# Two transformer layers in one kernel: order of the attention's small products, last down products row by row, first projections in two banks

## The chip, the cores and the metric

The kernel runs on one core of one Trainium2 chip. The metric is the device time of one execution in microseconds (us). Three runs of the kernel before took 1893.55, 1894.83 and 1896.32 us; the median is 1894.83. One further execution was recorded by the hardware profiler; all durations of single instructions come from it.

The core has five engines that run side by side and wait for each other through semaphores: PE multiplies matrices[...], DVE, ACT and POOL work elementwise, and SP issues DMA transfers.

## What is computed

Two layers, each with an attention-like part and a feed-forward part (FFN) that both read the same normalised input and are both added to x. The change touches the second layer only:

```
xn = _layernorm(x)
x = x + _L1_attn_ref(xn, ...) + _L1_ffn_ref(xn, ...)

# attention: b = 2, l = 1024, 16 heads of 32
qkv = x @ W_qkv.T + b_qkv
scores = einsum('bqhe,bkhe->bhqk', q, k) / sqrt(32), causal
attn = softmax(scores)
out = einsum('bhqk,bkhe->bqhe', attn, v) @ W_out.T + b_out

# FFN: 512 -> 2048 -> 512
h = silu(x @ w_gate) * (x @ w_up)
h_sparse = h with the two largest of each four |h| kept
out = h_sparse @ w_down
```

Everything is float32. A float32 product appears in the trace as two matmul instructions.

## The kernel before

The tokens are four blocks of 512 rows (`x1[0..3]`). The first layer ends at about 704 us; the second layer's attention runs from there to about 1283 us, its FFN to the end.

**Order of work.** Between `start = mark()` and `in_program_order(start)` (L1137 to L1154) each engine executes its instructions exactly in the order in which the Python code issues them. The same holds for the FFN from L1175 on. So moving a call in the Python code moves its instructions in every engine's queue.

**PSUM.** `ps_bank(name, which)` gives one of two single banks; `ps_wide(name)` gives one of three double banks, in strict rotation. A new tile waits until the last reader of the same bank or double bank is done.

**Projections.** `piece` (L826) builds a product of four chunks as two parts; its second part ends with `done`, which empties the bank: `project` (q and k) by ACT at L854, `values` by DVE at L872, `project_out` by DVE at L1027. The bank number is `(behind_steps or 1) % 2`. `behind_steps` is None until the attention's loop is over, so up to then every piece uses bank 1 (bank 0 holds the attention's output `o`); after the loop the two banks alternate. The first four pieces (L1133) run ahead of the loop.

**Attention.** A unit is a batch entry and a group of four heads, 8 units in all. The softmax needs each row's maximum first, so scores are computed twice: `maxima` (L881, tile `m`, rows on partitions) forms them 13 steps ahead, DVE adds the causal mask on the diagonal (L897) and reduces them to `tops` (L898). `larger` (L905) merges the two column halves of rows 512 to 1023. `shift_part` (L910) splits the negated maxima into three bf16 parts, and `shift_rows` (L922) turns them by four transposes on PE (tile `px`) and copies them with DVE (L932) into `neg`. `weights` (L934, tile `s`) forms the transposed scores (L943), adds `neg` by a product with ones (L949), takes the exponential on ACT (L960) and clears the masked corner on POOL (L965). `gather` (L974, tile `o`) multiplies with v (L985) and adds the weights up in `acc` (L993: POOL, from step 83 on DVE); it runs one step behind `weights`. When half j of a unit is done, `total` (L1000, tile `w`) sums `acc` over partitions by a product with ones, ACT copies the sum to `inv`, and `divide` (L1012) takes the reciprocal in four quarters on DVE and multiplies once on POOL (L1017).

The loop has 96 steps (12 per unit: 4 for j = 0, 8 for j = 1) and 13 ahead of them. One step n issues, in this order: `weights`; what is listed in `middle`; `gather` of the step before; (a projection part where n < 0); `maxima` of step n + 13; one projection part if one is ready; what is listed in `fixed`. For unit u, `shift_rows` is in `fixed` at 12u - 6 and 12u + 2, `larger` in `middle` at 12u - 1, `total` in `fixed` at 12u + 7 and 12u + 15, and its four `divide` one, one, two and three steps later.

**FFN.** Each of 8 groups has two gate-and-up units (`gate_up`), then `sparsify` (L1237: one ACT and eleven DVE instructions per half), then the down product. Seven groups use a 2x2 block scheme with seven products instead of eight (`down`, L1292, for each half of the rows; 8 matmul instructions of 256 columns each) whose inputs are sums: of weights by `down_weights` (POOL, L1219 to L1223; L1222 overwrites the quarter w12), of hidden values by `down_hidden` (DVE, L1232 to L1235). Several products of one half accumulate in the same bank, and DVE adds the bank to x1 between them (L1322). The last group uses plain row products, `row_down` (L1357: one block of 128 rows, 8 matmul instructions of 512 columns), which store their rows at once. Work that finds no place between the units is in `tail`: five products of the last-but-one group's half 0, all seven of its half 1, then the eight row products of the last group, with that group's `sparsify` steps (`some_steps`) in between.

Of the kernel before, what the change touches and what calls it, by code (L numbers as in the profile page):

```python
# [9 lines left out]
F32 = mybir.dt.float32  # L10
# [5 lines left out]
P = 128  # L16
B, S, D = 2, 1024, 512
N = B * S
TT = 512
# [16 lines left out]
def two_layers(ctx: ExitStack, tc: tile.TileContext, t: dict, out: bass.AP):  # L36
# [718 lines left out]
    with tc.tile_pool(name="b", bufs=1, reuse_waits="tile") as b:  # L755
# [67 lines left out]

        behind_steps = None

        def piece(name, lhs, rhs, done):  # L826


            got = []

            def part(n):
                if n == 0:
                    nonlocal behind_steps
                    if behind_steps is not None:
                        behind_steps += 1
                    got.append(ps_bank(name, (behind_steps or 1) % 2))
                for k in (2 * n, 2 * n + 1):
                    nc.tensor.matmul(  # L838
                        got[0], lhs(k), rhs(k), start=(k == 0), stop=(k == KC - 1)
                    )  # L840
                if n:
                    done(got[0])

            return [(part, 0), (part, 1)]
# [200 lines left out]

        rest, fixed, middle = [], {}, {}

# [3 lines left out]
        def put_mid(n, *what):  # L1051

            middle.setdefault(n, []).append(what)

        for u in range(len(units)):

            for half in range(2):
                n = per * u - ahead + (3, 11)[half]
                if half:
                    put_mid(n + 1, larger, u)  # L1060
                for m in range(3):
                    put_mid(n + 2 + m, shift_part, u, half, m)
                put(n + 4, shift_rows, u, half)
            if u:
                lo = per * (u - 2) if u > 1 else -ahead
                for x in range(4):
                    rest.append((lo, per * u - ahead - 1, project(u, x // 2, x % 2)))
            if u > 1:
                put(per * (u - 2) - 1, load_qk, units[u][1])
            for j in range(2):  # L1070
                put(min(per * u + 8 * j + 7, per * len(units) + 2), total, u, j)
        for x in range(4):
# [45 lines left out]
        def what_is_fixed(n):  # L1118
            for f, *args in fixed.pop(n, ()):
                f(*args)  # L1120
                if f == total:
                    for q in range(4):
                        put(n + 1 + (q * 2 // 3 if n < len(second) else 0), divide, *args, q)

# [8 lines left out]
        for x in range(4):  # L1133
            for f, *args in project(0, x // 2, x % 2):
                f(*args)
        behind = None
        start = mark()  # L1137
        for n in range(-ahead, len(second)):
# [3 lines left out]
            if behind is not None:  # L1142
                gather(*behind)
            behind = now
            if n < 0:
                one_part(n)
# [8 lines left out]
        gather(*behind)  # L1155
        behind_steps = 0
        n = len(second)
# [18 lines left out]
    with tc.tile_pool(name="c", bufs=1, reuse_waits="tile") as c_:  # L1176
# [34 lines left out]
        def down_weights(n, last):  # L1211
# [64 lines left out]
        held_d = {}  # L1276
        behind_units = False

        def bank_for(n, half, m):

            if not behind_units:
                return ps_bank(f"d{m}_{n}_{half}", (m + half) % 2)
            if m in (0, 3):
                held_d["pair"] = ps_wide(f"d{m}_{n}_{half}")
            return held_d["pair"][:, m in (1, 4), :]

        def residual(n, half, i, e):
# [4 lines left out]
        def down(n, half, m):  # L1292
# [3 lines left out]
            s2, s3, s4 = sd[n, half]  # L1296
            t1, t2, t4 = td[n]
# [59 lines left out]
        def row_down(n, i, j):  # L1357

            block = 2 * units[2 * n][0] + i
            bank = ps_bank(f"dr_{n}_{i}_{j}", i)  # L1360
            for r in range(4):
# [5 lines left out]
            nc.vector.tensor_add(x, x, bank)  # L1367
            row = block * TT + j * P
            nc.sync.dma_start(out=out[row : row + P, :], in_=x)

        for n in range(groups - 1):
# [6 lines left out]
            for last in range(2):  # L1378
                put1(u - 1, 3 + last, down_weights, n, last)
            for half, at in enumerate(((8, 11), ()) if end else (range(4, 11), range(11, 18))):  # L1380
                steps = list(sequence(n, half))
# [4 lines left out]
                tail += steps  # L1386
            put1(u, 3, down_hidden, n, 0)
            if not end:
# [24 lines left out]
        for n, (pb, g, half) in enumerate(units):  # L1413
# [33 lines left out]
            if n + 2 < len(units):  # L1447
                load_gu(n + 2)
        behind_units = True
        for f, *args in tail:  # L1450
# [73 lines left out]
```

## Time and profile before

The profiled execution took 1895.49 us; its span, from the first to the last instruction, is 1893.8 us, which leaves 1.7 us around it. Busy time in each stage, from the profile by windows:

| window (us) | what runs | PE busy | DVE | ACT | POOL | granted PE clock |
|---|---|---|---|---|---|---|
| 0 to 704 | first layer | 682.24 | 305.60 | 139.67 | 187.67 | 1.00 |
| 704 to 722 | first four projections | 14.80 | 0.45 | 2.52 | 0.00 | 1.00 |
| 722 to 1260 | attention's loop | 515.50 | 339.87 | 198.45 | 323.70 | 0.99 |
| 1260 to 1283 | last output projections | 23.00 | 7.77 | 0.58 | 6.22 | 1.00 |
| 1283 to 1824 | FFN units | 534.18 | 381.61 | 118.96 | 194.54 | 1.00 |
| 1824 to the end | tail | 55.65 | 36.74 | 5.04 | 6.71 | 0.91 |

PE is the busiest engine in every stage. Its idle time is largest in the tail, where it is busy for 55.65 of 70 us. The granted clock is the share of PE's full speed that the chip allowed; below 1.00 the same matmul takes longer.

### The profile page before, as it was taken

The numbers are of one execution on the slowest core, as the hardware profiler recorded it, in microseconds if no ns is written. First come the engines' busy times: TensorE is split into PE (matmuls) and PEld (weight loads), VectorE is DVE, ScalarE is ACT, GpSimd is POOL, SyncE is SP. The second block draws the span as 40 slices with busy tenths as digits, with TensorE's granted clock in tenths as the row PEclk, the third lists the DMA queues.
The fourth block names the chain that finished last, engine by engine and source line by source line (L and its number), as shares of the span: only waits on it lengthen the run. The fifth ranks groups of instructions, "written<-read, shape, count | busy, mean of one in ns | idle before, by whom it ended". The sixth has DMA issues, their size and how long they took to land.

```text
span 1893.8 us, 17968 instructions
## 1 busy us (share of the span) xinstructions
PE 1825.4 (96%) x6988; PEld 851.4 (45%) x6988; DVE 1072.0 (57%) x1430; ACT 465.2 (25%) x660; POOL 718.8 (38%) x638
## 2 busy tenths in 40 slices
PE   7999999999999999999999999899999999999988
PEld 4444444444444443333333333334455555555554
DVE  3774443334533235655666656652768678668664
ACT  2321121112221112334333333421212212211220
POOL 4222233114441101366667657732243344344310
PEclk9999999999999999999999999999999999999999
DMA  6121111001110100000000000011111102201001
GB/s 234 39 78 34 34 34 34 23 22 47 37 34 22 34 6 23 1 12 12 1 12 12 24 11 12 24 45 29 38 29 49 56 22 78 78 22 56 34 0 45
DMA packets 29460, 68.06 MB, mean 36 GB/s; under 512 B 3392, under 2 KB 11584, under 8 KB 27840
## 3 DMA queue, kind: packets, MB, share of 16 engines
q1 hardware_dynamic: 28656, 66.61, 11.0%
q8 instruction: 56, 0.92, 0.2%
q10 hardware_dynamic: 720, 0.30, 0.1%
q14 instruction: 28, 0.23, 0.0%
HBM read 62.70 MB, written 4.19 MB: 35 GB/s over the span
## 4 chain that ended last, share of the span: by engine, by line
PE 88%; DVE 5%; issue 2%; ACT 2%; POOL 1%; DMA 0%; SPq 0%; DVEq 0%; ACTq 0%; POOLq 0%
PE p_a L177 20%; PE p_c L177 19%; PE acc L621 12%; PE d L1308 9%; PE pq L838 6%; PE m L890 4%; PE s L943 4%; PE o L985 3%; PE po L838 2%; PE pv L838 2%; PE dr L1362 1%; DVE tops L898 1%; PE w L1005 1%; POOL acc L993 1%; DVE m L897 1%
## 5 line engine op out<-in xcount | busy, mean ns | idle before, releaser
L993 POOL TENSOR_TENSOR acc<-acc,pt 128x1024 f32<-128x1024 f32 (+3 forms) x138 | 233.7, 1715 | 0.0
L621 PE MATMUL acc<-w2h,h 128*128 128x512 f32 x512 | 230.1, 594 | 3.1 <-DVE y L533 1.8
L898 DVE TENSOR_REDUCE tops<-m 128x2 f32<-128x1024 f32 (+2 forms) x192 | 180.8, 955 | 59.3 <-PE m L890 54.7
L634 DVE TENSOR_TENSOR x<-x,acc 128x512 f32<-128x512 f32 x128 | 86.1, 685 | 174.6 <-PE acc L621 137.9
L960 ACT ACTIVATE pt<-s 128x1024 f32<-128x1024 f32 (+3 forms) x160 | 115.0, 766 | 180.5 <-PE s L949 172.6
L621 PEld LDWEIGHTS acc<-w2h,h 128*128 128x128 f32 x512 | 96.5, 190 | 123.1 <-issue 115.0
L838 PE MATMUL pq<-xt,wqk 128*128 128x512 f32 x256 | 129.2, 631 | 4.7 <-ACT qk L854 3.9
L897 DVE TENSOR_TENSOR m<-m,mask 128x256 f32<-128x256 f32 x128 | 54.7, 427 | 137.1 <-PE m L890 113.3
L1327 POOL TENSOR_TENSOR x<-x,de 128x512 f32<-128x512 f32 x42 | 67.9, 1630 | 149.4 <-DVE x L1322 117.6
L177 PE MATMUL p_a<-t_a,s_a 128*128 128x512 f32 x256 | 117.0, 601 | 2.0 <-DVE t_a L154 2.0
L177 PE MATMUL p_a<-xt,w 128*128 128x512 f32 x256 | 117.5, 602 | 0.7 <-ACT xt L134 0.7
L177 PE MATMUL p_c<-xt,s_c 128*128 128x512 f32 x256 | 115.2, 593 | 1.7 <-issue 1.1
L177 PE MATMUL p_a<-xt,s_a 128*128 128x512 f32 x256 | 115.3, 593 | 0.0
L177 PE MATMUL p_c<-xt,gu 128*128 128x512 f32 x256 | 114.9, 592 | 0.0
L177 PE MATMUL p_c<-t_c,s_c 128*128 128x512 f32 x256 | 114.6, 592 | 0.0
L943 PE MATMUL s<-qk,qk 32*128 32x512 f32 (+3 forms) x768 | 100.8, 537 | 10.0 <-DVE tops L898 10.0
L890 PE MATMUL m<-qk,qk 32*128 32x512 f32 (+3 forms) x768 | 103.4, 538 | 5.7 <-ACT acc L960 3.0
L1322 DVE TENSOR_TENSOR x<-x,d 128x512 f32<-128x512 f32 x70 | 47.8, 683 | 56.0 <-PE d L1308 56.0
L838 PEld LDWEIGHTS pq<-xt,wqk 128*128 128x128 f32 x256 | 44.8, 193 | 73.7 <-issue 61.3
L177 PEld LDWEIGHTS p_a<-t_a,s_a 128*128 128x128 f32 x256 | 48.6, 192 | 63.7 <-issue 62.1
L177 PEld LDWEIGHTS p_a<-xt,w 128*128 128x128 f32 x256 | 48.4, 193 | 64.0 <-issue 62.7
L965 POOL TENSOR_SCALAR_AFFINE_SELECT pt<-pt 128x256 f32<-128x256 f32 x112 | 47.6, 439 | 76.1 <-ACT pt L960 75.6
(226 smaller groups left out, 2797.5 us busy)
## 6 DMA issues: line engine op xcount, KB each, us to landing
w<-in_W SPq DMA_DIRECT2D x32, 512.0 KB, 3.6
gu<-in_gu SPq DMA_DIRECT2D x32, 512.0 KB, 3.5
wd<-in_down SPq DMA_DIRECT2D x8, 1024.0 KB, 4.9
x<-in_x SPq DMA_DIRECT2D x16, 256.0 KB, 4.4
w2h<-in_W2q SPq DMA_DIRECT2D x4, 1024.0 KB, 11.5
xr<-in_x SPq DMA_DIRECT2D x16, 256.0 KB, 2.6
wqk<-in_WqkvT SPq DMA_DIRECT2D x16, 256.0 KB, 3.3
out_x<-x SPq DMA_DIRECT2D x16, 256.0 KB, 2.0
```

Source lines behind the costliest of these rows:

```text
L177: nc.tensor.matmul(pair[:, m, :], a[:, m, k, :], x[:, k, :], start=start and k == 0, stop=stop and k == 1, skip_group_check=True,)
L621: nc.tensor.matmul(bank, h[:, m, j * P : (j + 1) * P], w2h[:, :, 2 * (n % NU) + m, :], start=(m == 0), stop=(m == 1 and not up),)
L634: nc.vector.tensor_add(r, r, bank)
L838: nc.tensor.matmul(got[0], lhs(k), rhs(k), start=(k == 0), stop=(k == KC - 1))
L890: nc.tensor.matmul(pair[h // 2][:, h % 2, :e], q[rows, qt * P : (qt + 1) * P], k[rows, c * 512 : c * 512 + e], start=True, stop=True,)
L897: nc.vector.tensor_add(d, d, mask.unsqueeze(1).to_broadcast([P, 2, P]))
L898: nc.vector.tensor_reduce(out=tops[u][:, c, qt, 2 * p : 2 * p + 2], in_=pair[p][:, :, :e], axis=mybir.AxisListType.X, op=ALU.max,)
L943: nc.tensor.matmul(pair[h // 2][:, h % 2, s:], k[rows, kt * P : (kt + 1) * P], q[rows, cols], start=True, stop=False,)
L960: nc.scalar.activation(pt[:, :, s:], pair[p][:, :, s:], AF.Exp, scale=1.0 / math.sqrt(HD))
L993: eng.tensor_add(acc[:, :, s:], acc[:, :, s:], pt[:, :, s:])
L1308: nc.tensor.matmul(out_[:, j, :], lhs[:, q, j * P : (j + 1) * P], rhs[:, q, :], start=m in (0, 1, 3, 4) and j == q == 0, stop=j == q == 1, ...
L1327: nc.gpsimd.tensor_add(r, r, held_d["u2"])
```

## The change

Four edits, all in the second layer.

1. The bank counter of the projections is renamed `alone`; it runs during the first four pieces too, is None during the loop, and starts again behind it.
2. The loop gets a third list, `after`, whose entries are issued straight behind `gather`. `shift_rows` moves there, one step later than before (12u - 5 and 12u + 3). `total` moves there in the same step as before. So both stand ahead of that step's `maxima`. `larger` moves from the middle of its step to its end. The four `divide` move one step forward, to the end of `total`'s own step, again that step, and the two steps behind. The last unit's second `total` and its `divide`, which come after the loop, stay.
3. The last-but-one FFN group gets a tile of its own for the sum t3 (`own_t3`), so that its weights stay unchanged, and half 1 of its rows is done by four plain row products instead of seven block products; `down_hidden` of that half falls away. The row products alternate with the five block products of half 0 in the tail.
4. `row_down` takes a double bank for two rows instead of the two single banks, and the block products in the tail take single banks instead of a double bank. Rows are stored only in a batch entry's last group.

```diff
-        behind_steps = None
+        alone = 0
...
-                    nonlocal behind_steps
-                    if behind_steps is not None:
-                        behind_steps += 1
-                    got.append(ps_bank(name, (behind_steps or 1) % 2))
+                    nonlocal alone
+                    if alone is not None:
+                        alone += 1
+                    got.append(ps_bank(name, 1 if alone is None else alone % 2))
...
                 if half:
-                    put_mid(n + 1, larger, u)
+                    put(n + 1, larger, u)
                 for m in range(3):
                     put_mid(n + 2 + m, shift_part, u, half, m)
-                put(n + 4, shift_rows, u, half)
+                put_after(n + 5, shift_rows, u, half)
...
             for j in range(2):
-                put(min(per * u + 8 * j + 7, per * len(units) + 2), total, u, j)
+                n = per * u + 8 * j + 7
+                if n < len(second):
+                    put_after(n, total, u, j)
+                    for q in range(4):
+                        put(n + q * 2 // 3, divide, u, j, q)
+                else:
+                    put(len(second) + 2, total, u, j)
...
-                        put(n + 1 + (q * 2 // 3 if n < len(second) else 0), divide, *args, q)
+                        put(n + 1, divide, *args, q)
...
-        behind = None
+        behind, alone = None, None
...
             behind = now
+            for f, *args in after.pop(n, ()):
+                f(*args)
             if n < 0:
                 one_part(n)
...
-        behind_steps = 0
+        alone = 0
...
-                nc.gpsimd.tensor_sub(w12, w22, w12)
+                if n < groups - 2:
+                    nc.gpsimd.tensor_sub(w12, w22, w12)
                 nc.gpsimd.tensor_sub(td[n][2], w21, td[n][1])
+
+        def own_t3(n):
+
+            td[n].append(c_.tile([P, 2, D // 2], F32, tag="td1", name=f"td3_{n}", bufs=2))
+            nc.gpsimd.tensor_sub(td[n][3], quarters_w(n)[3], quarters_w(n)[1])
...
-                held_d[half, m % 2] = bank_for(n, half, m)
+                held_d[half, m % 2] = ps_bank(f"d{m}_{n}_{half}", (m + half) % 2)
...
-            bank = ps_bank(f"dr_{n}_{i}_{j}", i)
+            if i == 0:
+                held_d["rows"] = ps_wide(f"dr_{n}_{j}")
+            bank = held_d["rows"][:, i, :]
...
-            row = block * TT + j * P
-            nc.sync.dma_start(out=out[row : row + P, :], in_=x)
+            if n % G == G - 1:
+                row = block * TT + j * P
+                nc.sync.dma_start(out=out[row : row + P, :], in_=x)
...
-            for half, at in enumerate(((8, 11), ()) if end else (range(4, 11), range(11, 18))):
+            for half, at in enumerate(((8, 11),) if end else (range(4, 11), range(11, 18))):
...
         n = groups - 1
+        rows = [(row_down, n - 1, i, j) for j in (2, 3) for i in range(2)]
         behind_last, tail = tail, [(some_steps, n, 0, 1)]
         for what in behind_last:
-            if what[0] == down and what[2:] == (1, 0):
-                tail.append((down_hidden, n - 1, 1))
-            tail.append(what)
-            if what[0] == down and what[2:] != (0, 2):
-                tail.append((some_steps, n, 0, 1))
-        tail.append((some_steps, n, 1, 1))
+            if what[0] == down:
+                if rows:
+                    tail += [rows.pop(0), (some_steps, n, 0, 1)]
+                tail += [what, (some_steps, n, 0, 1)]
+            else:
+                tail.append(what)
+        tail += [(some_steps, n, 0, 2), (some_steps, n, 1, 1)]
```

More of the change, by code (lines that the diff above doesn't have):

```diff
@@ L1041, in two_layers @@
         per, ahead = len(second) // len(units), 13
-        rest, fixed, middle = [], {}, {}
+        rest, fixed, middle, after = [], {}, {}, {}
         def put(n, *what):
@@ L1053, in put_mid, with put_after @@
             middle.setdefault(n, []).append(what)
+        def put_after(n, *what):
+            after.setdefault(n, []).append(what)
         for u in range(len(units)):
@@ L1276, in two_layers @@
         held_d = {}
[L1277 to L1285, printed above, removed]
         def residual(n, half, i, e):
@@ L1296, in down @@
             s2, s3, s4 = sd[n, half]
-            t1, t2, t4 = td[n]
+            t1, t2, t4, t3 = (td[n] + [t3])[:4]
             lhs, rhs = (
@@ L1387, in two_layers @@
             put1(u, 3, down_hidden, n, 0)
+            if end:
+                put1(u, 3, own_t3, n)
             if not end:
@@ L1448, in two_layers @@
                 load_gu(n + 2)
-        behind_units = True
         for f, *args in tail:
```

## The prediction

> **What bounds the kernel now.** First the page: busy shares, clock row and chain of waits.
>
> ```profile
> PE 1825.4 (96%) x6988; PEld 851.4 (45%) x6988; DVE 1072.0 (57%) x1430; ACT 465.2 (25%) x660; POOL 718.8 (38%) x638
> ...
> PE 88%; DVE 5%; issue 2%; ACT 2%; POOL 1%; DMA 0%; SPq 0%; DVEq 0%; ACTq 0%; POOLq 0%
> ```
>
> The chain is TensorE (PE) for 88% of the span; DMA has no share. So the change gains where PE stands still, or where it removes PE work. I then read PE's timeline at the three places it touches: the first projections, two steps of the attention, the end.
>
> **First projections.** PE's timeline (start, length, in brackets the idle time before and who ended it):
>
> ```profile
> 704.37 3.70 PE L838 MATMUL pq<-xt,wqk 128*128 128x512 f32 x8 [0.78 <-DVE x L634]
> 708.85 3.70 PE L838 MATMUL pq<-xt,wqk 128*128 128x512 f32 x8 [0.78 <-ACT qk L854]
> ```
>
> The pieces start 4.48 us apart (708.85 - 704.37; the fifth at 722.28), all in bank 1, each waiting for ScalarE to empty it. The work itself is 8 matmuls at 0.429 us (28 row products of L1362 take 12.28 us) = 3.43. With two banks in turn, pieces two to four and the first of the loop (bank 1, emptied one piece earlier) lose 4.48 - 3.43 = 1.05 each: **4 x 1.05 = 4.2 us**. The wait before the first piece, for DVE, stays. Behind it PE waits for less than 1.5 us in all up to 776.8, and the next load needed, wv, is issued at 636.0 and lands in 7.2 us, so nothing else is late. Bounds 3.1 to 4.2.
>
> **Attention.** I call step i of a unit its i-th of twelve (i = 0 to 3: j = 0, widths 512 to 128; 4 to 11: j = 1). Scores s and maxima m take two of three double banks each, in rotation; px (transposed maxima) and w (ones product) take one. Unit 2, steps 2 to 4:
>
> ```profile
> 918.41 0.39 PE L928 MATMUL px<-identb,parts 128*128 128x128 bf16 x4
> 918.73 0.49 PE L943 MATMUL s<-qk,qk 32*128 32x128 f32 x4
> 920.12 0.38 PE L943 MATMUL s<-qk,qk 32*128 32x128 f32 x2 [0.90 <-DVE tops L898]
> ...
> 924.16 1.06 PE L1005 MATMUL w<-acc,ones 128*32 128x512 f32 x8
> 925.15 1.14 PE L943 MATMUL s<-qk,qk 32*128 32x512 f32 x8
> ```
>
> px at the end of step 2 takes the double bank that would have been step 3's first, so the scores need both double banks of step 2's maxima; DVE empties the second only at 919.98. s and neg of width 128 need 0.52; here 918.73 to 920.60 passes, 1.35 too much.
>
> *Step 3 after.* Order s, neg, o, w, px, m, piece. From 918.41: 0.09 (change from the piece to s), s + neg 0.52, o 0.57; now w wants that second double bank and waits 0.53 until 920.12; w 0.90, px 0.40, m 1.08, piece 1.91. Sum 6.00, against 925.15 - 918.41 = 6.74: 0.74 gained. m's double banks are free by then: the exponentials end about 1.4 after s starts, inv's copy (0.58) about 0.9 after w ends, m's second half starts 0.53 after its first. Behind m stand the piece and step 4, whose neg the px copy (0.41 on DVE, now ahead of m's reductions) feeds in time. Seven units: 5.2.
>
> *Step 7 after.* From 940.43 to 947.18 are 6.75; the same sum with s 1.29, o 0.90 and no wait is 6.57: 0.19 each in units 0 to 5, 1.1. In unit 6 no piece covers px: it waits 0.37 for ScalarE and s 0.40 for DVE; moved, I get s(8) at 1198.0 for 1199.47: 1.45.
>
> *larger and the reciprocals (0.94 each).* They leave DVE's queue at step 11 (larger 1.0, one reciprocal), so step 0's scores get their bank earlier. In most units step 11's piece hides it, and the last o waits for POOL anyway. In unit 1, without a piece, 0.5. But the POOL multiplication (1.27) now stands ahead of step 10's mask:
>
> ```profile
> 899.06 0.77 POOL L965 TENSOR_SCALAR_AFFINE_SELECT pt<-pt 128x256 f32<-128x256 f32 x2
> 899.79 3.58 POOL L993 TENSOR_TENSOR acc<-acc,pt 128x768 f32<-128x768 f32 x2
> 903.33 1.27 POOL L1017 TENSOR_TENSOR att<-att,inv 128x512 f32<-128x512 f32 x1
> ```
>
> POOL runs without a pause here, so the mask comes at 900.3 to 901.1, o (at 900.65) loses up to 0.5, and the 0.48 that m waits next for DVE takes that up. POOL's later work keeps its time: 0, bounds 0 and 7 x 1.27 = 8.9 lost. In unit 7 no maxima are left and DVE does the sums; reciprocals ahead of sums and the multiplication ahead of two masks put the last o some 0.5 later (bounds -0.5, +1.2).
>
> Attention: 5.2 + 1.1 + 1.45 + 0.5 - 0.5 = **7.75 us**. No row shows w straight behind o; w before s costs 0.99 and o before m 1.00, so 0.90 may be 0.14 off either way at 15 places: +-2.
>
> **The clock.** Where PE waits long, the granted clock halves (the x columns hold instruction counts, the clock is third from the end):
>
> ```profile
> 1096.00:1100.00 4.00, 4.00 (x12) 1.36 (x14) 0.86 (x2) 0.00 (x0) 1.47 (x3) 0.50 0.00 0
> ...
> 1874.00:1878.00 4.00, 3.76 (x6) 1.62 (x7) 1.32 (x2) 0.00 (x0) 0.00 (x0) 0.64 0.18 63
> ```
>
> It happens at steps 11/0 of units 1 and 5 (840.9 and 1093.4) and twice at the end. From one o to the next takes 7.14 and 7.52 us there against 4.55 in unit 2: 2.6 and 3.0 us lost. [...] Here pauses of 2.40 (ahead of 1840.25) and 1.92 (ahead of 1874.24) did it, and 1.7 to 1.9 inside 3.4 us in units 1 and 5; 1.39 (ahead of 1222.39) did not. [...]those pauses fall to some 1.65 within 3.4 us (1.2 for the exponential behind POOL, 0.45 for the mask), near the edge. I count one of the two drops as gone: **2.8 us**, bounds 0 and 5.6.
>
> **The end.** PE's timeline:
>
> ```profile
> 1824.11 1.89 PE L1308 MATMUL d<-wd,h 128*128 128x256 f32 x8
> ...
> 1835.95 1.89 PE L1308 MATMUL d<-wd,h 128*128 128x256 f32 x8
> 1840.25 3.07 PE L1308 MATMUL d<-td,sd 128*128 128x256 f32 x8 [2.40 <-DVE sd L1234]
> 1844.19 3.75 PE L1308 MATMUL d<-wd,h 128*128 128x256 f32 x8 [0.88 <-DVE de L1319]
> ...
> 1857.90 1.88 PE L1362 MATMUL dr<-wd,h 128*128 128x512 f32 x4
> ```
>
> From 1824.11 twelve down products run, five of half 0 and seven of half 1, at 1.72 us pure (1825.83 - 1824.11); 20.6 of 33.8 us is work, the rest waits between products that share a bank, the wait for sd, and half clock. After: five products (8.6) and four row products of 3.43 (13.7), alternating, 22.3 us. A row product lies between any two products that share a bank, so the waits of 0.78 to 0.88 go; down_hidden (4 on DVE) goes with the 2.40. PE is through at 1846.4. What is late next is DVE's thinning of the last group: the last eviction from 0.38 behind PE (0.60), one step (0.61), the first L1266 (1.14) end at 1849.2, and the last group's row products start there instead of at 1857.90: 8.7. From there on the order is unchanged: 32.0 us to 1889.94, with 1.92 of waiting and a half-clock stretch (1.7). The pause of 2.8 ahead of it probably brings another such stretch, and the old one falls away half the time: 0.5 lost. **8.2 us**, bounds 5.5 and 10.5.
>
> Hidden: t3 in a tile of its own is the same POOL subtraction (1.26), moved from 1744.72 to behind 1774.81; POOL waits for PE at 1787.84 with 6.43 idle. The row pairs take double banks last read long before (the first, pb, by L201). No store is added: the last-but-one group stored nothing before either.
>
> **Sum.** 4.2 + 7.75 + 2.8 + 8.2 = 22.95. The profiled execution took 1895.49 (span 1893.8 and 1.7 around it), 0.66 above the median of 1894.83. 1895.49 - 22.95 = 1872.5.
>
> **Rivals.**
> - *POOL takes the attention's gain* (16 in 100). It runs without a pause from step 8 to step 0, and a saving on PE ahead of such a stretch counts only if the stretch starts earlier. Against: POOL idles 1.60 just ahead (887.81), waiting for the exponential, so it follows PE. Only 4.2 + 8.2 then: 1883.
> - *All clock drops vanish* (17): 2.8 more in the attention and 2.4 at the end: 1867.
> - *Slower: the multiplication blocks POOL's queue* (5). It waits for the fourth reciprocal; if that ends later than POOL's sums (899.1), mask, o and scores wait behind it[...]. At 1.3 + 2.8 in seven units that is 29 us, 6 more than all the gains: 1901. It decides from a fourth reciprocal about a microsecond behind POOL; by the trace it ends near 897.5, 1.6 ahead.
> - *It does not do what it says* (4): the pair counts as one tile, every second row waits for an eviction, and the attention's waits only move: 1895.
>
> The forecast has 58. Range 1863 to 1885: it holds the forecast with its bounds, all drops gone, and POOL's case. A measurement tells about 0.2% (3.8 us) from no change: faster 0.91, same 0.04, slower 0.05.
>
> **What would show it.** Right: projections 3.43 apart; no wait on tops ahead of the step-3 scores but about 0.5 ahead of w; the last group's row products starting some 9 us nearer to the attention's end, one pause of about 2.8 ahead of them. Wrong: PE waiting ahead of m for inv's copy, POOL waiting for reciprocals ahead of the masks, clock below 1.00 at more places than before.

## The result, and the profile after

The kernel after takes 1886.02 us (median of 12 runs, 1882.42 to 1889.2), beside 1901.99 us (1893.55 to 1906.84) for the kernel before in the same comparison: a ratio of 0.9926, 95% interval 0.9911 to 0.9942. It is faster, by 0.7% with an interval clear of 1, and lies 13.5 us above the forecast and 1 us outside its range. Where 22.95 us were forecast, 16.0 went by these medians. The profiled execution took 1882.42 us with a span of 1880.5; between the two profiled executions, from which the stages below are read, 13.3 us of span went.

The page of the kernel after, busy shares and chain of waits:

```profile
PE 1822.4 (97%) x6964; PEld 844.2 (45%) x6964; DVE 1067.7 (57%) x1424; ACT 464.8 (25%) x659; POOL 715.3 (38%) x635
...
PE 88%; DVE 4%; POOL 4%; ACT 2%; issue 2%; DMA 0%; SPq 0%; ACTq 0%; DVEq 0%; POOLq 0%
```

By this count 3 us of PE's busy time went and 10 of its idle time. That does not say what was gained: a matmul at half clock counts as busy (at 1343.57 us PE is busy for 3.41 of 3.41 us at a granted clock of 0.50), and so does a stall that the modelled end of the matmul before covers (0.4 us inside the row of m below, which carries no bracket). POOL's share of the chain rose from 1% to 4%, and DVE's fell from 5% to 4%. Stage by stage, from PE's timelines:

| stage | before (us) | after (us) | forecast gain | measured gain |
|---|---|---|---|---|
| up to the first weighted product | 776.79 | 772.29 | 4.2 | 4.5 |
| attention, from there to the FFN's first product | 505.66 | 499.25 | 10.55 | 6.4 |
| FFN units | 541.66 | 544.17 | 0 | -2.5 |
| tail, to the end of PE's last row product | 65.83 | 60.93 | 8.2 | 4.9 |

**First projections**, PE's timeline after (start, length, in brackets idle time and releaser):

```profile
703.97 15.80 PE L838 MATMUL pq<-xt,wqk 128*128 128x512 f32 x36
719.70 0.50 PE L890 MATMUL m<-qk,qk 32*128 32x128 f32 x8
```

Four pieces and the loop's first half piece run without a gap; the first maxima start at 719.70, where 724.20 was before. From the first piece to the first weighted product take 72.42 us before and 68.33 after, so 4.1 of the stage's 4.5 us are the change's; the other 0.4 come from the first layer, whose code is the same.

**Attention**, unit 2, step 3 after, first PE, then ACT:

```profile
911.38 1.06 PE L1005 MATMUL w<-acc,ones 128*32 128x512 f32 x8 [0.48 <-DVE tops L898]
912.37 0.40 PE L928 MATMUL px<-identb,parts 128*128 128x128 bf16 x4
912.70 1.56 PE L890 MATMUL m<-qk,qk 32*128 32x512 f32 x8
914.20 1.98 PE L838 MATMUL pq<-xt,wqk 128*128 128x512 f32 x4
```

```profile
912.50 0.59 ACT L1010 COPY inv<-w 128x512 f32<-128x512 f32 x1 [1.49 <-PE w L1005]
```

The wait of 0.48 ahead of w is there as forecast. But from m's start to the piece's are 1.50 us, not 1.08: w, px and m's two halves take four double banks from a rotation of three, so m's second half gets w's again, and ACT empties that only at 913.09. A regular unit went from 61.90 to 61.83 us. The 6.4 us came from elsewhere: before, units 1 and 5 were 4.8 and 5.0 us longer than a regular unit, after they are not. Units 0 and 4 became 0.7 and 1.2 us longer, because the wait between two units now stands ahead of the next unit's first scores and counts to the unit before: 1.03 us ahead of 833.57, for an exponential that itself waited for POOL's sums. Together these four units are 8.2 us shorter.

**The clock**, windows of the kernel after (columns: length, busy time of PE, PEld, DVE, ACT, POOL with counts, granted clock, DMA). The first two lie where unit 1 begins, the third where unit 5 begins, the last two in the FFN:

```profile
832.00:836.00 4.00, 2.68 (x31) 1.27 (x30) 2.64 (x6) 1.43 (x3) 4.00 (x5) 1.00 0.01 2
836.00:840.00 4.00, 4.00 (x30) 1.59 (x32) 2.15 (x4) 1.70 (x4) 4.00 (x7) 1.00 0.01 4
1080.00:1084.00 4.00, 2.69 (x30) 1.24 (x28) 2.38 (x6) 1.20 (x2) 4.00 (x5) 1.00 0.34 115
...
1342.00:1346.00 4.00, 2.49 (x7) 1.98 (x7) 3.93 (x5) 1.44 (x3) 0.42 (x1) 0.70 0.00 0
1346.00:1350.00 4.00, 4.00 (x10) 1.85 (x9) 3.81 (x5) 2.20 (x3) 0.00 (x0) 0.88 0.00 0
```

PE pauses for about 1.3 us of 4 at units 1 and 5 and keeps the full clock; both half-clock stretches of before are gone in this execution. One has appeared in the FFN, around pauses of 0.29 and 1.51 us that the kernel before has too.

**Tail**, PE's timeline after:

```profile
1840.87 5.37 PE L1372 MATMUL dr<-wd,h 128*128 128x512 f32 x8 [2.63 <-issue]
1847.02 7.13 PE L1372 MATMUL dr<-wd,h 128*128 128x512 f32 x16 [0.78 <-DVE x L1377]
1854.93 3.70 PE L1372 MATMUL dr<-wd,h 128*128 128x512 f32 x8 [0.78 <-DVE x L1377]
1860.55 3.70 PE L1372 MATMUL dr<-wd,h 128*128 128x512 f32 x8 [1.92 <-DVE h L1284]
1865.03 7.13 PE L1372 MATMUL dr<-wd,h 128*128 128x512 f32 x16 [0.78 <-DVE x L1377]
1872.94 3.70 PE L1372 MATMUL dr<-wd,h 128*128 128x512 f32 x8 [0.78 <-DVE x L1377]
```

Before, the rows stood in single banks and ran on:

```profile
1860.04 12.28 PE L1362 MATMUL dr<-wd,h 128*128 128x512 f32 x28 [0.27 <-DVE h L1266]
1874.24 15.70 PE L1362 MATMUL dr<-wd,h 128*128 128x512 f32 x32 [1.92 <-DVE h L1266]
```

The last group's rows start 25.16 us into the tail (1840.87 - 1815.71; the forecast's step gives 25.1). But now the second row of every pair waits 0.78 us for the eviction of the first, though it goes to the other bank of the pair. PE's row is 3.43 when another follows and 3.70 when it stops, so each such wait costs 0.78 + 0.27 = 1.05: 4.2 us in four pairs.

### The profile page after: what moved, and what is told of

Its sections match the earlier page's. It is cut to its first block, busy times and chain, and to the rows that moved or that the text cites. A ratio compares the mean times of both kernels' runs of the same rounds, so it can differ in the third digit from the quotient of the medians.

```text
span 1880.5 us, 17921 instructions
## 1 busy us (share of the span) xinstructions
PE 1822.4 (97%) x6964; PEld 844.2 (45%) x6964; DVE 1067.7 (57%) x1424; ACT 464.8 (25%) x659; POOL 715.3 (38%) x635
## 4 chain that ended last, share of the span: by engine, by line
PE 88%; DVE 4%; POOL 4%; ACT 2%; issue 2%; DMA 0%; SPq 0%; ACTq 0%; DVEq 0%; POOLq 0%
PE p_a L177 20%; PE p_c L177 19%; PE acc L621 12%; PE d L1316 8%; PE pq L838 6%; PE m L890 4%; PE s L943 3%; PE o L985 3%; POOL acc L993 3%; PE pv L838 3%; PE dr L1372 2%; PE po L838 2%; PE w L1005 1%; PE pp L480 1%; DVE tops L898 1%
## 5 line engine op out<-in xcount | busy, mean ns | idle before, releaser
L838 PE MATMUL pq<-xt,wqk 128*128 128x512 f32 x256 | 124.6, 615 | 0.8 <-ACT qk L854 0.8
L1335 POOL TENSOR_TENSOR x<-x,de 128x512 f32<-128x512 f32 x39 | 62.9, 1628 | 141.7 <-DVE x L1330 120.7
L890 PE MATMUL m<-qk,qk 32*128 32x512 f32 (+3 forms) x768 | 107.5, 533 | 3.6 <-ACT acc L960 3.0
L943 PE MATMUL s<-qk,qk 32*128 32x512 f32 (+3 forms) x768 | 93.4, 532 | 3.2 <-ACT pt L960 2.3
L985 PE MATMUL o<-pt,v 128*32 128x512 f32 (+3 forms) x640 | 70.1, 477 | 4.3 <-POOL pt L965 4.0
```

What stands on the lines that cost most here:

```text
L838: nc.tensor.matmul(got[0], lhs(k), rhs(k), start=(k == 0), stop=(k == KC - 1))
L890: nc.tensor.matmul(pair[h // 2][:, h % 2, :e], q[rows, qt * P : (qt + 1) * P], k[rows, c * 512 : c * 512 + e], start=True, stop=True,)
L943: nc.tensor.matmul(pair[h // 2][:, h % 2, s:], k[rows, kt * P : (kt + 1) * P], q[rows, cols], start=True, stop=False,)
L985: nc.tensor.matmul(po[rows, s:], v[:, rows], pts[h // 2][:, h % 2, s:], start=(kt == 0), stop=last, tile_position=(0, h * HD),)
L1335: nc.gpsimd.tensor_add(r, r, held_d["u2"])
```

## The experiments

A mean granted clock stands with each ratio, and beside it that of before. The runs were timed in three comparisons, each with executions of before of its own, and before's mean clock differs between them, so only the two of one row are compared. (For the comparison of the result no clock of before was kept.)

| kernel | ratio to before (95%) | attention (us) | FFN units | tail | mean clock | before's beside it |
|---|---|---|---|---|---|---|
| before | 1 | 505.66 | 541.66 | 65.83 | | |
| after, first | 0.9926 (0.9911 to 0.9942) | 499.25 | 544.17 | 60.93 | 0.9934 | |
| after, again | 0.9933 (0.9908 to 0.9957) | 503.19 | 544.14 | 60.93 | 0.9933 | 0.9915 |
| two_banks_only | 0.9972 (0.9958 to 0.9987) | 506.79 | 541.65 | 61.29 | 0.9912 | 0.9915 |
| recip_only | 0.996 (0.9944 to 0.9977) | 503.19 | 541.65 | 61.28 | 0.9945 | 0.9904 |
| end_only | 0.9976 (0.9959 to 0.9993) | 518.23 | 542.49 | 60.93 | 0.9916 | 0.9904 |
| att_undone | 0.9972 (0.9961 to 0.9984) | 506.20 | 542.49 | 60.93 | 0.9917 | 0.9923 |
| div_late | 0.995 (0.993 to 0.997) | 506.43 | 542.49 | 60.94 | 0.9928 | 0.9923 |
| filled | 0.9965 (0.9942 to 0.9988) | 499.99 | 541.66 | 62.82 | 0.9943 | 0.9904 |
| rows_single | 0.9918 (0.9894 to 0.9943) | 502.80 | 544.20 | 55.05 | 0.9942 | 0.9923 |
| px_first | 0.9903 (0.988 to 0.9927) | 495.24 | 544.17 | 60.94 | 0.9943 | 0.9923 |
| shared_pair | 0.997 (0.9958 to 0.9981) | 506.46 | 543.96 | 61.03 | 0.9939 | 0.9915 |
| mended | 0.9878 (0.9857 to 0.9899) | 499.55 | 543.35 | 55.05 | 0.994 | 0.9915 |
| fused | 0.9887 (0.9864 to 0.991) | 497.67 | 544.83 | 56.85 | 0.9937 | 0.9904 |

The stage columns come from one profiled execution each and hold its half-clock stretches. To compare them I take off what these cost: over windows of 2 us, the sum of 2 x (1 - granted clock). It overstates the loss where PE was idle in the stretch, so it is good to about 1 us: without these losses the four traces with before's attention code have 498.3 to 499.5 us of attention, and the three with after's 498.1 to 499.4.

### The end: is a pair of banks one tile?

```diff
-            if i == 0:
-                held_d["rows"] = ps_wide(f"dr_{n}_{j}")
-            bank = held_d["rows"][:, i, :]
+            if n == groups - 1:
+                bank = ps_bank(f"dr_{n}_{i}_{j}", i)
+            else:
...
```

> The last group's eight row products take single banks in turn instead of the two halves of a double bank; nothing else differs from the kernel after. Theory (a double bank is one tile to the order of the program, so the second row of a pair waits for the eviction of the first: 4 waits of 0.78 us plus a refill of about 0.27, 1.05 each): the 0.78 us waits on the eviction at the row products are gone, the alternating part keeps its length, and the end from the tail's start is 4.2 us shorter than after's 60.9, so about 56.7; against before about 0.990. Rival (the waits come of the eviction's own pace on VectorE, whatever the banks are): the same waits stand at the same rows, the end stays at 60.9 +- 0.3 and the ratio at 0.993.

PE's timeline of rows_single at the end:

```profile
1846.66 13.97 PE L1375 MATMUL dr<-wd,h 128*128 128x512 f32 x32 [2.63 <-issue]
1862.55 14.00 PE L1375 MATMUL dr<-wd,h 128*128 128x512 f32 x32 [1.92 <-DVE h L1284]
```

Four rows run without a break, then the wait for the sparsified h, then four more. The tail is 5.88 us shorter than after's: 4.2 for the four waits and 1.7 for a half-clock stretch that this execution doesn't have. The theory holds; the eviction's pace is not the limit. (Its attention is 3.55 longer than after's by half-clock stretches worth 3.42, at code that is the same.)

### The maxima's second half: which copy does it wait for?

```diff
         def put_after(n, *what):
-            after.setdefault(n, []).append(what)
+            if what[0] == shift_rows:
+                after.setdefault(n, []).insert(0, what)
+            else:
+                after.setdefault(n, []).append(what)
```

> In the kernel after, the transposition of the maxima is issued ahead of the ones-product wherever both stand in one step, so that the second half of the maxima waits for VectorE's copy of the transposed maxima and no longer for ScalarE's copy of the inverse sums. Theory (after's maxima take 1.50 to 1.57 us instead of 1.08 because their second half wants the double bank that ScalarE is still copying out of): maxima back to about 1.1 us in the steps that have both, 0.42 us in each of some 15 steps, so about 6 us less than after in attention; against before about 0.990. Rival (the wait moves: the transposition, now first, waits 0.5 us or more for the maxima's parts on ScalarE or VectorE, and the ones-product's copy ends as late for whoever wants that bank next): the sum of the step stays within 0.1 us, and the ratio at 0.993.

Unit 2, step 3 of px_first, PE's timeline:

```profile
910.38 0.38 PE L928 MATMUL px<-identb,parts 128*128 128x128 bf16 x4 [0.48 <-DVE tops L898]
910.69 1.07 PE L1005 MATMUL w<-acc,ones 128*32 128x512 f32 x8
911.68 1.14 PE L890 MATMUL m<-qk,qk 32*128 32x512 f32 x8
```

m is back at 1.08 us (911.68 to the piece at 912.76), and the 0.48 wait has only changed hands. Regular units take 61.10 us, 0.73 less than after's and 0.80 less than before's; step 3 lost 0.44 and step 7 0.30. Attention without half-clock losses is 493.5 us, where after has 499.25.

Two kernels then put w and px in the two halves of one double bank. The first leaves the order of the copies as it is:

```diff
-            px = ps_wide(f"px_{u}_{half}")[:, 0, :].bitcast(BF16)
+            pair = both_in.pop("pair", None)
+            if pair is None:
+                pair = ps_wide(f"px_{u}_{half}")
+            px = pair[:, 1, :].bitcast(BF16)
```

(`total` leaves its double bank in `both_in`.)

> The kernel after, with the ones-product and the transposed maxima of one step in the two halves of one double bank instead of in two double banks. Theory (what costs after its attention gain is that the step takes four double banks of a rotation of three, so the maxima's second half gets the bank of the ones-product before ScalarE has copied it): with three taken in the step, the maxima are back at 1.1 us and regular units at 61.0 or less; if the 0.48 us wait ahead of the ones-product goes as well, at 60.1. Attention 5.5 to 12 us shorter than after's 499.25, ratio 0.987 to 0.990. Rival (the rotation shifted by one makes the maxima of the neighbouring steps wait for the two evictions of the shared double bank): the wait stands in the steps behind instead, regular units within 0.3 of 61.83, ratio 0.993.

PE's timeline of shared_pair in the same step; the transposition now shows the tile name w:

```profile
912.48 1.06 PE L1010 MATMUL w<-acc,ones 128*32 128x512 f32 x8 [0.48 <-DVE tops L898]
914.24 0.38 PE L931 MATMUL w<-identb,parts 128*128 128x128 bf16 x4 [0.69 <-ACT inv L1015]
914.55 1.14 PE L890 MATMUL m<-qk,qk 32*128 32x512 f32 x8
```

Neither expectation came true. m is at 1.07 as the theory said, but px now waits for ACT's copy out of the *other* half, 0.69 us plus the refill, and regular units take 62.48 us. It is the end's case again: in both, the write to one half came after an access to the other half that the program had issued earlier (0.78 us there, 0.69 here). So it should vanish if the program issues both products first and the two copies behind them. `fused` does that, on top of `mended` below, with w ahead of px again:

> The kernel called mended, but with the ones-product and the transposed maxima in the two halves of one double bank, both products issued ahead of both copies out of it. Theory (a double bank is one tile: in the run with a shared double bank the second product waited 0.69 us for the copy of the first half, only because that copy stood ahead of it in the program): no such wait, maxima at 1.1 us, regular units 61.0 +- 0.2 like mended's 61.1; time within 2 us of mended's 1874.9. Rival (the wait for VectorE's reductions ahead of the pair grows, as the rotation of double banks is one shorter): regular units at 61.8 or more.

PE's timeline of fused:

```profile
913.97 1.06 PE L1016 MATMUL w<-acc,ones 128*32 128x512 f32 x8 [0.48 <-DVE tops L898]
914.97 0.40 PE L931 MATMUL w<-identb,parts 128*128 128x128 bf16 x4
915.29 1.14 PE L890 MATMUL m<-qk,qk 32*128 32x512 f32 x8
```

No wait between the three; regular units take 60.98. But the profiled FFN and tail are longer than mended's by 1.5 and 1.8 us. The tail has a half-clock stretch that mended's has not. The FFN's part is one wait, where the tail begins:

```profile
1817.30 3.70 PE L1388 MATMUL dr<-wd,h 128*128 128x512 f32 x8 [1.31 <-DVE e_c L231]
```

shared_pair has the same wait of 1.31 us, and mended, whose attention takes a double bank for each product, has none. A shared pair in fourteen steps leaves the rotation two places further back, so the tail's first row pair gets a double bank that DVE is still reading. The median of fused, 1877.69, is 2.8 us above mended's and so outside the 2 us that were expected; the intervals overlap.

### Attention's gain: which part, and is it work or clock?

Taking the attention edit back as a whole, and taking back the reciprocals alone:

> The kernel after with the attention edit taken back (transposed maxima, ones-product, larger and reciprocals at their places of before); first projections in two banks and the FFN's end stay. Theory (the gain of 6.4 us in attention is nearly all the two half-clock stretches of units 1 and 5, 5 us each, less 1.8 in units 0 and 4, and the regular units gain only 0.06): regular units 61.9; [...]with both stretches about 505.5 in attention and a time of 0.996 of before, without them about 496, and 0.991. Rival (the moved order itself is worth the predicted 7.75 us): attention is 7 us longer than after's whatever the clock shows.

> In the kernel after, the four reciprocals of a half unit go one step later each, to the places they had before; the rest of the attention edit stays. Theory (POOL's multiplication, released by the reciprocals, now runs ahead of a mask that an exponential's successor waits for: +0.67 and +1.15 us in units 0 and 4, up to 1.9 in units 6 and 7): these waits on POOL and on the exponential behind it are gone and attention is 2 to 4 us shorter than after's 499.25 from the first weighted product to the FFN's start; regular units stay at 61.83. Rival (the waits belong to the order of transposed maxima and ones-product): the waits stay, and attention is within 0.5 us of after's. Third: the half-clock stretches of units 1 and 5 come back (+2.5 us each) as the reciprocals' places gave them away.

```diff
-                        put(n + q * 2 // 3, divide, u, j, q)
+                        put(n + 1 + q * 2 // 3, divide, u, j, q)
```

att_undone has 506.20 us of attention, 6.95 more than after's, which by the bare number is the rival's forecast. But its half-clock stretches cost 6.8, so without them it has 499.4: the same. div_late, which keeps the moved products, has 506.43, of which 8.5 are half clock, so its third theory came true. Its PE timeline where unit 1 begins:

```profile
831.60 0.50 PE L890 MATMUL m<-qk,qk 32*128 32x128 f32 x8 [0.25 <-DVE tops L898]
831.90 1.13 PE L943 MATMUL s<-qk,qk 32*128 32x512 f32 x4
833.91 0.99 PE L943 MATMUL s<-qk,qk 32*128 32x512 f32 x2 [0.88 <-DVE tops L898]
...
838.03 3.45 PE L838 MATMUL pq<-xt,wqk 128*128 128x512 f32 x4
```

A reciprocal stands on DVE (831.97, 0.94 us) ahead of the mask and the reductions that free the scores' bank. The waits on POOL that its first theory wanted gone are gone there, but these stand in their place. The 2 to 4 us did not come: without half clock attention is 497.9, no further below after's 498.1 to 499.4 than the estimate is good for. One part can be read: the last three steps of unit 7, from the scores of step 9 to the end of the last o, take 13.03 us in after and 11.83 in div_late, as in before. So the early reciprocals cost 1.2 us there. The opposite edit, the reciprocals alone moved in the kernel before:

```diff
-                        put(n + 1 + (q * 2 // 3 if n < len(second) else 0), divide, *args, q)
+                        m = n + (q * 2 // 3 if n < len(second) else 1)
+                        if m == n:
+                            divide(*args, q)
+                        else:
+                            put(m, divide, *args, q)
```

> The kernel before with the reciprocals alone moved one step earlier, behind the ones-product of the same step. Theory (of the attention edit only this part gains: VectorE is free for the maxima's reductions at the first step of units 1 and 5): the waits of 1.22 us for the reductions there are gone or below 0.6, a wait for the exponential behind POOL of about 1.0 comes in their place, the half-clock stretches are shorter or gone (3.4 us each); ratio about 0.9965. Rival (the reciprocals at the earlier place keep VectorE waiting for ScalarE's copy of the sums, with the maxima's reductions queued behind them): each of 14 steps loses 0.3 to 1 us, and the time is not below before's.

PE's timeline of recip_only at the same place:

```profile
840.15 0.50 PE L890 MATMUL m<-qk,qk 32*128 32x128 f32 x8
841.67 1.28 PE L943 MATMUL s<-qk,qk 32*128 32x512 f32 x6 [1.02 <-ACT pt L960]
```

Before had two waits there, for the reductions:

```profile
837.10 0.50 PE L890 MATMUL m<-qk,qk 32*128 32x128 f32 x8 [0.23 <-DVE tops L898]
839.74 0.70 PE L943 MATMUL s<-qk,qk 32*128 32x512 f32 x2 [1.22 <-DVE tops L898]
```

They are replaced by one for the exponential, as in the kernel after. PE's work is the same and regular units still take 61.9, yet the median falls by 0.4% and the mean clock rises from 0.9904 to 0.9945. (The profiled execution has two stretches in units 6 and 7, 3.4 us.) Whether the clock is the cause shows when nothing is made faster. `filled` adds work to the kernel before:

```diff
+                if h == 2 and (u, j, kt) in ((1, 0, 0), (5, 0, 0)):
+                    spare = ps_bank(f"spare_{u}", 1)
+                    nc.tensor.matmul(spare, q[:, :P], k[:, :512], start=True, stop=True)
                 nc.tensor.matmul(
                     pair[h // 2][:, h % 2, s:], k[rows, kt * P : (kt + 1) * P], q[rows, cols],
```

> The kernel before, with one extra multiplication (128 rows, 512 columns, about 1 us, its result unread) put into PE's pause of 1.2 us between the first and the second pair of heads of the first weighted product of units 1 and 5. Everything that the attention computes stays. Theory (attention's gain in the kernel after is the clock's: the edit cuts PE's one long pause at these two places into shorter ones, and the 3.4 us that each half-clock stretch costs are saved): with the pause filled the clock stays at 1.00 at both places and attention is 5 to 7 us shorter than before's 505.7, the time about 0.9965 of before's, though no engine does less. Rival (the stretches do not follow the pause): they stay, and the time is that of before or up to 1 us more.

PE's timeline of filled, and its windows at the two places:

```profile
839.86 1.12 PE L945 MATMUL spare<-qk,qk 128*128 128x512 f32 x2
841.15 0.70 PE L946 MATMUL s<-qk,qk 32*128 32x512 f32 x2 [0.16 <-DVE tops L898]
```

```profile
838.00:842.00 4.00, 3.59 (x28) 1.39 (x22) 3.75 (x8) 0.56 (x2) 4.00 (x6) 1.00 0.02 6
842.00:846.00 4.00, 4.00 (x28) 1.49 (x24) 2.15 (x4) 2.52 (x4) 4.00 (x7) 1.00 0.00 0
1092.00:1096.00 4.00, 4.00 (x28) 1.70 (x24) 2.15 (x4) 2.17 (x4) 4.00 (x7) 1.00 0.00 0
```

Two useless products, one in each unit, keep the clock at 1.00, and attention is 5.67 us shorter with no work taken away. Over the timed executions the mean clock rises from 0.9904 to 0.9943. So what the half-clock stretches cost there is shown: without the two, attention gains 5.67 us net of the spare products. In the kernel after, 6.8 of the 8.2 us that units 0, 1, 4 and 5 gained are half clock by the windows.

### The kernel after once more, and the other two parts

> The kernel after itself, unchanged, beside the others of this call. Theory: the FFN's half-clock stretch (1.67 us, in the kernels with first projections and attention as after has them) [...]its place and number differ from one execution to the next: another trace of the same code may show one stretch more or fewer, and times between 1882 and 1889. Rival (the stretch belongs to the code): the same stretch at 1342 to 1348 us, and attention of 499.25 +- 0.1.

Its windows in attention and the FFN:

```profile
836.00:840.00 4.00, 3.75 (x29) 1.67 (x27) 2.10 (x4) 2.52 (x4) 4.00 (x5) 0.70 0.02 6
...
1212.00:1216.00 4.00, 3.35 (x16) 1.02 (x20) 2.59 (x4) 1.44 (x3) 2.25 (x7) 0.64 0.00 0
...
1242.00:1246.00 4.00, 2.77 (x10) 1.13 (x11) 3.46 (x5) 0.13 (x1) 3.15 (x5) 0.73 0.86 315
...
1348.00:1352.00 4.00, 2.49 (x7) 1.88 (x7) 3.97 (x4) 1.44 (x3) 0.54 (x1) 0.70 0.00 0
```

The same code has three stretches in attention in this execution, none in the other, and a span 6.1 us longer. The stretch in the FFN came back at the same place in it, so neither expectation holds alone: att_undone and div_late, with the same FFN code, take 542.49 there and don't have it.

What tells the traces with the stretch from those without it can be read at this place. Within each execution the half-clock stretches start whole multiples of 3.413 us apart: in the kernel after at 1343.57 and 1841.92, 146 of them; in the kernel before at 840.85 and 1093.43, 74. So the changes of the clock in a trace lie on a grid of 3.413 us, and measured from the span's start it lies elsewhere in each execution. The two pauses in the FFN, 0.29 and 1.51 us, are the same to 0.01 us in all fourteen traces. Windows laid on that grid, two of the kernel after and one of before:

```profile
1340.16:1343.57 3.41, 1.61 (x6) 0.38 (x4) 3.41 (x4) 1.01 (x1) 1.28 (x1) 1.00 0.10 38
1343.57:1346.98 3.41, 3.41 (x7) 2.49 (x8) 3.31 (x5) 2.31 (x2) 0.00 (x0) 0.50 0.00 0
```

```profile
1352.85:1356.26 3.41, 1.90 (x8) 1.44 (x8) 3.38 (x4) 0.85 (x3) 0.49 (x1) 1.00 0.00 0
```

In after both pauses fall into one window, 1.80 us of idle time together, and the next runs at half clock; in before only the longer one does, 1.51, and the clock stays. In all six traces with the stretch one window there holds 1.77 to 1.81 us of idle time; in the eight without it none holds more than 1.57. That limit is this place's only: at units 1 and 5 of before windows with 1.22 and 1.14 us lost the clock, and in rows_single's tail one with 1.98 kept it. What decides in general was not shown.

> The kernel before with the one change that the first projections alternate between two banks. Theory: the gain of 4.5 us in the first projections is independent of the rest: PE reaches the first maxima at 719.7 instead of 724.2; the half-clock stretches in attention and at the end may shift. Ratio 0.9976 if they stay, 0.995 to 0.999 with one fewer or more. Rival (the removed gaps come back in the next step, where the maxima wait for ScalarE's copies of the projections): the first weighted product starts no more than 2 us earlier than before's 776.79.

The first weighted product starts at 772.82, 3.97 us earlier than before's: the gain holds alone. This kernel's end is the code of before and takes 61.29 us, not 65.83: before's profiled tail held half-clock stretches worth 5.1, this one none.

> The kernel before with the FFN's end of the kernel after (row by row in double banks), attention and first projections as before. Theory: the end is 60.9 +- 1.8 us from the tail's start to PE's last row instead of 65.8, and the FFN 0.85 longer (VectorE's step beside POOL's subtraction): together 2.3 to 5.9 us, ratio 0.997 to 0.9988. Rival [...]: no gain.

The profiled execution of end_only has 18.8 us of half-clock loss in attention, so only its FFN and tail are read: 0.83 longer and 4.90 shorter than before's, of which the half-clock stretches are 3.4 (5.1 before, 1.7 here). Both are as expected. Its median is 4.6 us below before's.

### What is mended

> The kernel after with three things mended: the transposed maxima ahead of the ones-product, single banks for the last group's row products, and the subtraction for the last half group's weights on POOL one unit later, behind the steps of the sparsification on VectorE. Theory: attention 495.2 as with the first alone, or 493.8 without its one half-clock stretch; FFN 0.85 shorter (the wait of 1.40 us for VectorE's copy back to 0.55); end 55 to 56.7 instead of 60.9. The sum, from after's 1882.4: -4.0 -0.85 -5 = about 1872.5, ratio 0.987. Rival for the third (POOL's subtraction meets another step of VectorE later in the unit): the FFN stays at 542.5 without the half-clock stretch, 544.2 with it.

The third edit moves one entry: `put1(u + 1, 0, own_t3, n)` instead of `put1(u, 3, own_t3, n)`. The wait in the FFN, in the kernel after and in mended:

```profile
1784.71 3.67 PE L177 MATMUL p_c<-xt,s_c 128*128 128x512 f32 x8 [1.40 <-DVE e_c L221]
```

```profile
1785.55 3.67 PE L177 MATMUL p_c<-xt,s_c 128*128 128x512 f32 x8 [0.56 <-DVE e_c L221]
```

0.84 us, as expected. In the kernel after, POOL's subtraction (L1241, 2.25 us) pushed POOL's next two sums back, so that the second of them still ran when DVE's `both` (L1277) started, which then took 1.75 us. Alone, `both` takes 0.68 (the same line in rows_single's tail) and the subtraction 1.28 (in mended). The median of mended is 1874.85 us, 22.7 below before's 1897.55 in that comparison: better than both kernels, and about what had been forecast for the change.

## Why the prediction was wrong

- **First projections, 4.2:** right, 4.1 (and 0.4 from the first layer).
- **Attention, 7.75 for the order of the work:** the failed step. Without half clock, attention has 498.8 us before and 499.25 after: nothing gained. The wait ahead of the scores went and the 0.48 ahead of w came as worked out. The term that failed is "m's double banks are free by then": it set w's copy beside m's start, but m's second half is the third double bank after w's and starts ahead of the copy's end. That cost 0.44 us in step 3 and 0.30 in step 7 of each regular unit, about 4.9 in all. With px first, a regular unit gives 0.80 of the forecast 0.93, and attention 5.3 of the 7.75. The list of signs for "wrong" had named PE waiting ahead of m for inv's copy.
- **Unit 6 and unit 7:** steps 6 and 7 of unit 6 took 11.71 us before, 11.27 after and 10.98 in px_first, so 0.4 and 0.7 were gained where 1.45 was forecast. In unit 7 the early reciprocals and the multiplication behind them lost 1.2 us, where 0.5 was allowed; div_late and recip_only show that it is these. A further 0.6 of the profiled pair is a single DVE operation of 3.72 us in unit 6, which after_again does not have.
- **The clock, 2.8 of a possible 5.6:** a size. In the profiled pair both stretches of attention went, 6.8 us by the windows, and 1.7 came in the FFN. Over many executions it is the mean clock that counts: 0.9915 for before and 0.9933 for after in the comparison that holds both, which over 1890 us is 3.4 us and near the forecast. The way to it was in part luck. The prediction read 1.7 to 1.9 us of pauses within 3.4 us at units 1 and 5; by PE's busy time the most is 1.45 and 1.63. Around the pause at 1222.39, which kept the clock and for which it counted 1.39 alone, it is 1.62. So length alone did not separate them. That pauses of this size can cost clock was right: in before the granted clock was 0.50 from 840.85 and from 1093.43, and with the pauses filled it was 1.00 at both places.
- **The end, 8.2:** two terms. The rows start where the sum put them, but "from there on the order is unchanged: 32.0" left out that the two rows of a pair share one tile; that costs 4.2. And the baseline had been an execution whose tail lost 5.1 to half clock; the same code takes 61.3 without. With the pair split the gain is 61.3 - 55.05 = 6.2 without any stretch. The sentence on waits "between products that share a bank" named the cause wrongly for five of the seven waits: before's d products used the two halves of a pair, and only the sixth product of each half adds to the bank that was just read. The other five were the same effect, and could have told of it. The rival "the pair counts as one tile" had the right mechanism, with a price far too high.
- **own_t3, "hidden":** POOL had the idle time, but DVE did not: 0.85 us.

Together: 4.5 - 0.4 + 6.8 + 4.9 - 2.5 = 13.3, the measured difference of the spans (first stage, order of the work, its clock, tail, FFN).

## What to carry to other kernels

Before counting a bank as free, list every access that the program issued to its tile: a double bank handed out in halves is one tile, and a write to one half waited here for an earlier read of the other (0.78 us in each row pair). Follow the rotation past the moved instruction to whoever gets its bank next, however far behind that is. Price a pause of PE over several executions, not from one trace: whether the FFN's two pauses of 0.29 and 1.51 us cost clock went with whether both fell into one window of the 3.413 us grid (1.77 us or more together). Breaking one long pause can gain as much as the work moved (ratio 0.996 in recip_only), and even useless products can pay (0.9965 in filled).

## What the runs showed of the hardware

The granted clock of PE fell to 0.50 at 840.85 and 1093.43 in before, where PE had been idle for 1.22 and 1.14 us of the 3.41 us ahead, and both stretches lasted 6.83 us. Away from the trace's ends the stretches lasted one, two or once (in end_only) three times 3.413 us, for about 1.7 us of loss each time, and started whole multiples of 3.413 us apart within an execution. Pauses of 1.03 and 0.25 us at unit 1 kept the clock in one execution of the kernel after and lost it in the other, at the same code; in attention the two had none and three stretches. Pauses of 0.29 and 1.51 us in the FFN drew a stretch in six of the fourteen traces, those in which at least 1.77 us of them fell into one such window. On DVE, four operations with two float32 inputs took 1.64 to 2.3 us beside POOL's elementwise work (the kernel after, 1766.54 to 1774.32) where the same lines take 0.68 to 1.23 without, and POOL's three took 2.19 to 2.25 where such a one takes 1.27. Both were slower there, so idle time of one of them was not free.
